# A residual attention block in fp32: the order of work in the front, before the loop reaches its steady state

## The chip, the cores and the metric

The kernel runs on one core of a Trainium2 chip. A core has five engines that work through their own lists of instructions in order and wait for one another by semaphores: TensorE (PE, with its weight loads shown as PEld), VectorE (DVE), ScalarE (ACT), GpSimd (POOL) and SyncE (SP), which here issues nearly all DMAs. The metric is the device time in microseconds (us); lower is better. "Span" is the part of a profiled execution between its first and its last instruction.

## The reference

There are 64 batches of 128 tokens with 512 features, all in fp32. Each batch goes through multi-query attention with 16 heads of width 64 and one shared key and value head, a learned null key and value, an additive bias per head and a mask; the result is projected, normed and added to the input.

```python
xn = layernorm(x, g_in)
q = (xn @ Wq).reshape(b, n, H, DH).transpose(0, 2, 1, 3) * scale
kv = xn @ Wkv
k, v = kv[..., :DH], kv[..., DH:]
k = concatenate([null_k, k]); v = concatenate([null_v, v])
sim = einsum('bhid,bjd->bhij', q, k) + bias      # null_attn_bias in column 0
sim = where(causal_mask, neg, sim); sim = where(mask_p, sim, neg)
attn = softmax(sim, axis=-1)
out = einsum('bhij,bjd->bhid', attn, v)
out = layernorm(out.reshape(b, n, INNER) @ Wo, g_out)
return x + out
```

## The kernel before

The order of the work is written out by hand: every engine executes its instructions in the order in which the program names them, and a tile's buffer is taken over when its last reader is done. The program is a front followed by `for n in range(-6, B - 1): step(n)` (L1222). A step works on several batches at once, each at another stage. In step n the q products of a group of four batches, the keys and values of batch n+6, the scores of batch n+2, the exponentials of batch n+1 and the attention times values of batch n are formed, and for older batches the output product, norm and residual.

**The front.** The loads of x_0 to x_3, of the gain vector, of wq in four parts and of wkv are issued first (L161 to L173). `norm_stats(m)` (L239) takes mean and variance on VectorE and the power of -0.5 on GpSimd; `norm_apply(m)` (L249) applies them, on VectorE for the first four tiles and on ScalarE afterwards (with a small product "nmr" on VectorE ahead of it); `norm_T(m)` (L261) makes four transposes on TensorE and a copy on ScalarE. `keep_busy(k)` (L1188) issues k products of the identity with itself, whose results nobody reads; each shows as two instructions in the profile. `weights_q(kc)` (L842) scales a quarter of wq by the gain, `weights_kv_prod(kc)` (L862) multiplies it by the null key on GpSimd, and `weights_kv(kc)` (L871) scales wkv and reduces that product to 16 further columns. `causal(u)` (L195) writes a large negative number into the bias where a key lies ahead of a query, on GpSimd. `load_bias(0)` writes rows that `causal(1)` has filled, so it waits for it. `aTb` (L224) is the buffer of the transposed attention; it is cleared once.

**The groups.** The first group's q is formed by plain products (`q_plain`, L370) in steps -6 to -3. From step -2 on, the next groups use a scheme with 7 products in place of 8: `weight_sums` and `weight_sum_3` (L384, L389) form sums of blocks of wq, `token_sum` (L392) sums of blocks of the transposed tokens on GpSimd, and `product`, `keep` and `q_out` (L406, L431, L435) multiply and put the parts together through the PSUM tiles "a", "c" and "w". In step -4 the keys and values of the first three batches are formed at once (L1180).

**Scores to values.** `bias_add(b)` (L458) puts bias plus mask into the tile S[b] on GpSimd, `null_copy` adds the two null columns, `scores` (PE) and `scores_add` (DVE) the products of q and k. `scores_max`, `exps`, `rinv` and `scale` are the softmax in two halves, on DVE, ACT, DVE and POOL. S has two buffers, so `bias_add(n+2)` can't start before S[n] was read by the transposes. For batches 0 and 1 these are done by TensorE (`attn_T_pe`, L606), for later ones by VectorE and DMAs. `values` (L647) starts the product with v; with it goes a one-element copy "done" on VectorE that later PE work waits for, and `values_end` finishes it. `out_mm(0)` (L689) is the plain output product of batch 0; `out_weight_sum` (L721) forms sums of wo's blocks on GpSimd in steps 0 to 3.

**DMAs.** `load_second` (L175), `load_bias(0)`, the mask and x loads inside the steps, and `load_late` (wo and the output gain, L209) go through SP's queue in program order. An x load waits until its buffer is free, and what stands behind it waits too.

Of the kernel before, what the change touches and what calls it, by code (L numbers as in the profile page):

```python
# [8 lines left out]
FP = mybir.dt.float32  # L9
# [8 lines left out]
def kernel(  # L18
# [59 lines left out]
    nc = tc.nc  # L78
# [60 lines left out]
    def load_mask(g):  # L139
        m8s[g] = gp.tile([P, TOK], U8, tag="m8", name=f"m8_{g}")  # L140
        nc.sync.dma_start(
            out=m8s[g],
            in_=mask[g * GB : (g + 1) * GB].rearrange("b n -> (b n)").partition_broadcast(P),
        )
# [28 lines left out]
    )  # L173

    def load_second():  # L175
        nc.sync.dma_start(out=nbh, in_=null_bias.partition_broadcast(P))
        nc.sync.dma_start(out=nvb, in_=cond[1].partition_broadcast(P))
        load_mask(0)
        for m in (4, 5, 6):
            load_x(m)  # L180
        load_bias(1)
        for r in range(2):
            nc.sync.dma_start(
                out=nv2[r * DH : (r + 1) * DH, :], in_=cond[1].unsqueeze(1)
            )

    def load_bias(u):
        rows = slice(u * DH, (u + 1) * DH)
        bias_r = attn_bias.rearrange("(u f r) i j -> u r i f j", u=2, r=2)[u]
        for r in range(2):  # L190
            rf = slice(r * NF, (r + 1) * NF)
            nc.sync.dma_start(out=biasp[rows, rf, 0:NL], in_=bias_r[r, 0:DH, :, 0:NL])
            nc.sync.dma_start(out=biasp[rows, rf, NL:], in_=bias_r[r, DH:N])
# [193 lines left out]
        nc.vector.tensor_tensor(s4, a12, s2, ALU.subtract)  # L387

    def weight_sum_3():  # L389
        nc.gpsimd.tensor_tensor(s3, a11, a21, ALU.subtract)  # L390

    def token_sum(g, k):  # L392

        xS[g, k] = gp.tile([P, GB // 2, HK, N], FP, tag=f"xS{k}", name=f"xS{k}_{g}", bufs=1)
        lo, hi = xT[g][:, 0 : GB // 2], xT[g][:, GB // 2 :]
        b11, b12 = lo[:, :, lo_k], hi[:, :, lo_k]
        b21, b22 = lo[:, :, hi_k], hi[:, :, hi_k]
        p, m = {
            1: (b12, b11),
            2: (b22, xS.get((g, 1))),  # L400
            3: (b22, b12),
            4: (b21, xS.get((g, 2))),
        }[k]
        nc.gpsimd.tensor_tensor(xS[g, k], p, m, ALU.subtract)  # L404
# [26 lines left out]
    def keep(tag, name):  # L431
        kept[name] = bp.tile([P, HT], FP, tag=f"k{name}", name=f"k{name}", bufs=1)
        nc.scalar.copy(kept[name], prod[tag])  # L433
# [26 lines left out]
    def bias_add(b):  # L460
        g, t = divmod(b, GB)
        if b in (B3 + 1, B3 + 4):
            S[b] = gp.tile([P, R8, ROW], FP, tag="xT", name=f"s_{b}")
        else:
            S[b] = sp.tile([P, R8, ROW], FP, tag="s", name=f"s_{b}")
        nc.gpsimd.tensor_tensor(  # L466
            S[b][:, :, 1 : ROW - 1],
            biasp,
            mneg[g][:, t].unsqueeze(1).broadcast_to([P, R8, NL + N]),
            ALU.add,  # L470
        )

    def null_copy(b):
        g, t = divmod(b, GB)
        nc.gpsimd.tensor_copy(  # L475
            S[b][:, :, 0 : ROW : ROW - 1],
            nv[g][:, t, DH:].rearrange("p (k e) -> p e k", k=2),
        )
# [58 lines left out]
    def rinv(b, hf):  # L537
        rinvs[b, hf] = small.tile([P, R8], FP, tag="rinv", name=f"rinv_{b}_{hf}")
        nc.vector.reciprocal(rinvs[b, hf], rsum[b][:, hf])
# [246 lines left out]
    def pair_pow(b):  # L786
        nc.gpsimd.tensor_tensor(yn[b][1], yn[b][1], nhalf, ALU.pow)
# [52 lines left out]


    def weights_q(kc):  # L842
        if kc < 2:
            nc.vector.tensor_scalar(
                wq[:, kc, :], wq[:, kc, :], gin8[:, kc : kc + 1], None, ALU.mult
            )
        else:
            nc.scalar.activation(
                wq[:, kc, :], wq[:, kc, :], AF.Copy, scale=gin8[:, kc : kc + 1]
            )  # L850
# [9 lines left out]
            )  # L860

    def weights_kv_prod(kc):  # L862
        prods[kc] = sp.tile([P, H, DH], FP, tag="s", name=f"prod_{kc}")
        nc.gpsimd.tensor_tensor(
            prods[kc],
            wq[:, kc, :].rearrange("p (h d) -> p h d", d=DH),
            nkb.unsqueeze(1).broadcast_to([P, H, DH]),
            ALU.mult,
        )
# [9 lines left out]
    def step(n):  # L879
        def ok(b, end=B):  # L880
            return 0 <= b < end

        qg, part = divmod(n + 6, GB)
        mkv, mk, mb = n + 6, n + 5, n + 11
        mns = [m for m in (n + 10, n + 12) if ok(m) and (m >= 2 * GB) == (m == n + 12)]
        q, f = ok(qg, NG), part
        last_g, last_f = divmod(n + 5, GB)
        fast, last = q and qg > 0, 0 < last_g < NG
# [21 lines left out]
        if second:  # L910
            if n != B3 + 1:
                out_sums(p5673)
        elif ok(nb) and n >= 0 and n != 1:
            bias_add(nb)
            null_copy(nb)
        if third:
            pair_pow(p4)
        for m in mns:
            norm_stats(m)
        if fast and f == 0 and fill:  # L920
            for k in range(1, 5):
                token_sum(qg, k)
            if n == -2:
                weight_sum_3()
        if n == -4:
            bias_add(0)
            bias_add(1)
        if ok(nb) and n < 0:
            null_copy(nb)
        if n == B3:  # L930
            blocks_T(B3 + 1)
            blocks_move(B3 + 1)
        if third:
            out_product(p4, 4, ps_y, "X", start=False)
        if one:

            out_mm(n - 1, 0, NF if n > B3 + 1 else NC)
            if n == 1:
                attn_T_pe(1)
                bias_add(nb)  # L940
                null_copy(nb)
                out_stats(0)
        if fast:
            if f == 0:
                q_tile(qg)
# [5 lines left out]
            scores_max(B3 + 1, 0)  # L951
        if last:
            product(last_g, last_f, 4, ps_q, "a", start=False)
        if soft:
            exps(eb, 0, 0, 4)
        if third:
            out_part(p4 + 1, 0, "X")
        if last:
            q_out(last_g, HC + last_f, lo_t, "a")
            product(last_g, last_f, 3, ps_q, "c", start=False)  # L960
            q_out(last_g, last_f, hi_t, "c", "u2")
        if n == B3 - 1:
            scores(B3 + 1, 1)
            scores_add(B3 + 1, 1)
            scores_max(B3 + 1, 1)
        if third:
            pair_stats(p4 + 1)
        if 2 * GB <= mb < B:
            tokens_T(mb)
            if (mb + 1) % GB == 0:  # L970
                tokens_out(mb // GB)
        if soft:
            exps(eb, 0, 4)
        if fast and f == 0 and not fill:
            token_sum(qg, 1)
        if soft and n != B3 + 1:
            rinv(eb, 0)
            scale(eb, 0)
        if third:
# [20 lines left out]
            product(qg, f, 2, ps_w, "w")  # L1000
        elif q and not fast:
            q_plain(qg, 2 * f)
        if soft:
            exps(eb, 1, 0, 2)
        if third and n != B3:
            pair_norm(p4)
# [19 lines left out]
        elif first:  # L1026
            out_keep("X", "yp1", "p1")
            out_product(p12, 2, ps_w, "w")
            out_part(p12, 0, "w", "yp1")
        if soft:  # L1030
            exps(eb, 1, 2, 4)
        if soft and not second:
            exps(eb, 1, 4, 6)
# [34 lines left out]
                mask_neg(qg)  # L1068
            out_part(p5673, 1, "Y", "yu2")
        if ok(n + 1) and fill:  # L1070
            exps(n + 1, 1)
        if one and n == 1:
            residual(0)
        if n == B3 - 1:
# [2 lines left out]
        if sc and n != B3:  # L1077
            scores(nb, 0)
            scores_add(nb, 0)
            if ok(n + 1) and fill:  # L1080
                rinv(n + 1, 1)
                scale(n + 1, 1)
        split = sc and n != B3
        if n == B3:
            pair_nmr(p4 + 1)
        if ok(n):
            values(n, split)
        if third and n != B3:
            pair_residual(p4 + 1)
            store(p4 + 1)  # L1090
# [4 lines left out]
        if not ok(n) and fast:  # L1095
            product(qg, f, 6, ps_q, "a", start=False)
            keep("a", "u2")
        if ok(n) and not split:
            values_end(n, split)
            if n > B3 + 1:  # L1100
                out_mm(n - 1, NF)
# [6 lines left out]
            store(p4 + 1)  # L1108
            scores_max(nb, 0)

        late = first and fast
        if sc:
            scores(nb, 1)
            scores_add(nb, 1)
            if not late:
                scores_max(nb, 1)
        if ok(n) and split:
# [50 lines left out]
            kv_out(mkv, pk[:, 0:KVN])  # L1168
        if ok(mk) and not ok(mkv):
            kT_out(mk, k_T(mk))  # L1170
        if n == -1:
            attn_T_pe(0)
        if n == B3 - 2:
            bias_add(B3 + 1)
            null_copy(B3 + 1)
# [17 lines left out]


    nc.vector.tensor_scalar(gin8, gin, DH**-0.5, None, ALU.mult)
    norm_stats(0)
    norm_stats(1)
    norm_apply(0)
    norm_T(0)
    norm_stats(2)  # L1200
    norm_apply(1)
    norm_T(1)
    norm_stats(3)
    norm_apply(2)
    norm_T(2)
    keep_busy(8)
    norm_apply(3)
    norm_T(3)
    keep_busy(10)
    load_second()  # L1210
    weights_q(2)
    weights_q(0)
    weights_q(3)
    weights_q(1)
    nc.gpsimd.memset(aTb, 0.0)
    for kc in range(2):
        weights_kv_prod(kc)
    nc.vector.tensor_scalar(vnb[:, 0:DH], nvb, -1.0, None, ALU.mult)
    null_order(vnb[:, DH:], nbh)
    causal(1)  # L1220
    load_bias(0)
    for n in range(-6, B - 1):  # L1222
        step(n)
        if n == -6:
            for kc in range(2):
                weights_kv(kc)
            for kc in range(2, KC):
                weights_kv_prod(kc)
            load_late()
        if n == -5:  # L1230
            for kc in range(2, KC):
                weights_kv(kc)
            causal(0)
            mask_neg(0)
            weight_sums()

    load_res(B - 1)
    store(B - 3)
# [47 lines left out]
```

## Time and profile before

| | |
|---|---|
| median of 3 runs | 1126.49 us (1124.78 to 1126.77) |
| profiled execution | 1125.21 us |
| its span | 1123.4 us |
| PE busy | 1086.8 us (97%) |
| DVE, ACT, POOL busy | 806.8, 678.2, 745.0 us |
| first q product on PE starts | 17.97 us |
| first product of step -2 on PE starts | 55.92 us |
| out_mm(0) in step 1 starts | 93.81 us |

In lists of waits, a row reads "engine, what waited, line <- engine, what released it, line: us in total, times, longest us". In the timeline a row is: start in us, length in us, engine, line, operation, tile written <- tiles read, shape, number of instructions merged into the row, and in brackets the idle time before it and what ended it. Overlapping starts in one queue are normal, since a row's length runs to the end of its last write. Tiles carry the program's names: x the tokens, pxT their transposes, xT the copy of these, pq and pa, pc, pw products for q, pk and pkv those for keys and values, ps scores, paU and paL the transposed attention, po the values, py the output.

### The profile page before, as it was taken

The page shows a single profiled execution, that of the slowest core. Times are in us where ns is not written, and L with a number is a line of the kernel's source. Part 1 is how long each engine was busy: PE and PEld are TensorE (multiplying, and loading weights), DVE is VectorE, ACT ScalarE, POOL GpSimd, SP SyncE. Part 2 cuts the span into 40 slices and gives each one's busy share as a digit, 9 for nine tenths or more (in the row PEclk, how much of TensorE's full clock was granted, in tenths as well). Part 3 has the DMA queues.
Part 4 walks back from the last instruction along what each step waited for, and adds up shares of the span by engine and source line. Part 5 has one row for each costly group of instructions (what it writes and reads, how often), then busy time and mean ns, then how long its engine had stood idle before and what let it go on. Part 6 is the DMA issues. An engine that isn't in the chain of part 4 may idle for free.

```text
span 1123.4 us, 27505 instructions
## 1 busy us (share of the span) xinstructions
PE 1086.8 (97%) x9780; PEld 872.6 (78%) x9780; DVE 806.8 (72%) x1741; ACT 678.2 (60%) x2710; POOL 745.0 (66%) x588
## 2 busy tenths in 40 slices
PE   6888999999999999999999999999999999999987
PEld 4465788888888888888888888788888888888643
DVE  6564677786787777778777777877777886666762
ACT  2345656666675666676565667566567756657661
POOL 5454877667675676767577676657768575777832
PEclk9999999999999999999999999999999999999999
DMA  6313244353444435345343634534353453422333
GB/s 186 123 33 97 66 132 122 88 163 97 136 127 126 118 91 169 101 125 135 123 123 92 167 104 125 130 120 117 101 163 103 127 134 108 104 77 77 96 104 103
DMA packets 107864, 130.09 MB, mean 116 GB/s; under 512 B 29264, under 2 KB 72528, under 8 KB 105936
## 3 DMA queue, kind: packets, MB, share of 16 engines
q1 hardware_dynamic: 106480, 126.96, 40.1%
q8 instruction: 78, 1.28, 0.5%
q10 hardware_dynamic: 1248, 1.38, 0.4%
q14 instruction: 58, 0.48, 0.1%
HBM read 54.86 MB, written 31.46 MB: 77 GB/s over the span
## 4 chain that ended last, share of the span: by engine, by line
PE 82%; DVE 4%; DMA 4%; ACT 3%; POOL 2%; SPq 2%; issue 1%; ACTq 0%; POOLq 0%; DVEq 0%
PE pa L422 17%; PE pyX L750 16%; PE pyY L750 8%; PE pc L422 8%; PE ps L495 8%; PE po L636 7%; PE pk L308 5%; PE pw L422 4%; PE pyw L750 4%; PE py L697 3%; ACT s L522 2%; DMA x<-in_x_dram 2%; SPq L601 2%; DMA nbh<-cond_null_attn_bias_dram 1%; POOL xS L404 1%
## 5 line engine op out<-in xcount | busy, mean ns | idle before, releaser
L522 ACT ACTIVATE s<-s,nmax 128x65 f32<-128x65 f32 (+1 forms) x1024 | 372.1, 368 | 0.4
L466 POOL TENSOR_TENSOR s<-biasp,mneg 128x1536 f32<-128x1536 f32 x64 | 221.1, 3456 | 109.5 <-DVE sb L575 98.1
L543 POOL TENSOR_TENSOR s<-s,rinv 128x512 f32<-128x512 f32 (+1 forms) x128 | 189.3, 1480 | 119.3 <-DVE nmro L794 91.4
L680 ACT ACTIVATE oT<-po,nv 128x512 f32<-128x512 f32 x128 | 81.1, 684 | 199.4 <-PE po L636 199.4
L522 ACT ACTIVATION_READ_ACCUMULATOR s<-s,nmax 128x1 f32 x1024 | 194.6, 190 | 0.0
L750 PE MATMUL pyX<-wT,oT 128*128 128x256 f32 x696 | 164.7, 379 | 0.5 <-DVE kyu L762 0.5
L750 PEld LDWEIGHTS pyX<-wT,oT 128*128 128x128 f32 x696 | 131.8, 190 | 19.6 <-DVE kyu L762 0.9
L495 PEld LDWEIGHTS ps<-kT,qT 64*64 64x64 f32 x4096 | 94.5, 135 | 46.4 <-DVE s L508 24.2
L508 DVE TENSOR_TENSOR s<-ps,s 128x512 f32<-128x512 f32 (+1 forms) x128 | 121.5, 949 | 9.0 <-PE ps L495 8.7
L422 PE MATMUL pa<-xS,wq 128*128 128x256 f32 x480 | 123.7, 380 | 2.0 <-POOL wq L390 1.0
L513 DVE TENSOR_REDUCE nmax<-s 128x8 f32<-128x520 f32 (+1 forms) x128 | 120.1, 939 | 5.1 <-POOL s L475 3.7
L495 PE MATMUL ps<-kT,qT 64*64 64x64 f32 (+1 forms) x4096 | 118.9, 252 | 3.8 <-DVE s L508 3.1
L636 PE MATMUL po<-aTb,vs 64*64 64x256 f32 (+1 forms) x1240 | 118.5, 382 | 2.3 <-DVE done L668 2.2
L575 DVE STREAM_TRANSPOSE sb<-s 128x1536 f32<-128x1536 f32 x62 | 110.0, 1774 | 12.9 <-POOL s L543 3.6
L433 ACT COPY ku<-pa 128x256 f32<-128x256 f32 x120 | 44.8, 373 | 93.2 <-PE pa L422 93.2
L422 PEld LDWEIGHTS pa<-xS,wq 128*128 128x128 f32 x480 | 86.7, 190 | 12.3 <-ACT ku L433 1.6
L308 PE MATMUL pk<-wkv,xT 128*128 128x144 f32 x488 | 69.9, 286 | 0.0
L443 DVE TENSOR_TENSOR qT<-pw,kp 128x256 f32<-128x256 f32 x60 | 25.4, 424 | 61.4 <-ACT kp L433 61.3
L422 PE MATMUL pa<-xS,wS 128*128 128x256 f32 x240 | 67.8, 405 | 0.0
L636 PEld LDWEIGHTS po<-aTb,vs 64*64 64x64 f32 (+1 forms) x1240 | 57.0, 135 | 12.8 <-issue 3.9
L246 POOL TENSOR_TENSOR rstd<-rstd,nhalf 128x1 f32<-128x1 f32 x64 | 35.8, 560 | 42.9 <-DVE rstd L245 42.8
L422 PE MATMUL pc<-xS,wS 128*128 128x256 f32 x240 | 61.9, 380 | 1.9 <-POOL xS L404 1.9
(120 smaller groups left out, 2101.1 us busy)
## 6 DMA issues: line engine op xcount, KB each, us to landing
aTb<-sb SPq DMA_DIRECT2D x369, 64.0 KB
x<-in_x_dram SPq DMA_DIRECT2D x64, 256.0 KB
res<-in_x_dram SPq DMA_DIRECT2D x64, 256.0 KB
out_dram<-y SPq DMA_DIRECT2D x64, 256.0 KB
aTb<-sb SPq DMA_DIRECT2D x492, 32.0 KB
xd<-xb SPq DMA_DIRECT2D x14, 1024.0 KB
xT<-xd SPq DMA_DIRECT2D x56, 256.0 KB
wo<-in_L_cond_Wo_dram SPq DMA_DIRECT2D x1, 2048.0 KB
```

The lines of the kernel that those rows point to most:

```text
L308: nc.tensor.matmul(pkv, xT[g][:, t, kc, :], wkv[:, kc, :], start=(kc == 0), stop=(kc == KC - 1),)
L422: nc.tensor.matmul(prod[tag], w[:, kc, f * P : (f + 1) * P], t[:, :, kc, :], start=(start and kc == 0), stop=(kc == HK - 1), skip_group_ch ...
L466: nc.gpsimd.tensor_tensor(S[b][:, :, 1 : ROW - 1], biasp, mneg[g][:, t].unsqueeze(1).broadcast_to([P, R8, NL + N]), ALU.add,)
L495: nc.tensor.matmul(pv[u * DH : (u + 1) * DH, r, f, :], qT[g][rows, f, t, hf, u], kT[b][rows, 0:nk], start=True, stop=True,)
L508: nc.vector.tensor_tensor(sv, pss.pop((b, hf)), sv, ALU.add)
L513: nc.vector.tensor_reduce(nmax[b][:, hf], S[b][:, :, WITH_NULL[hf]], AX.X, ALU.max, negate=True)
L522: nc.scalar.activation(row, row, AF.Exp, bias=nmax[b][:, hf, k : k + 1], accum_out=rsum[b][:, hf, k : k + 1],)
L543: nc.gpsimd.tensor_tensor(sv, sv, rinvs.pop((b, hf)).unsqueeze(2).broadcast_to([P, R8, sv.shape[2]]), ALU.mult,)
L575: nc.vector.transpose(sb.rearrange("p j e q -> p e j q"), S[b][:, :, 1 : ROW - 1].rearrange("p e (j k) -> p e j k", k=Q),)
L636: nc.tensor.matmul(pos[b][u][r * DH : (r + 1) * DH, half], vals[keys, b % GB, 0:DH], aT_of(b)[keys, slots, r * NF : (r + 1) * NF], start=s ...
L680: nc.scalar.activation(oT[b][:, u * NF : (u + 1) * NF, :].rearrange("p f (s q) -> p s f q", q=Q), po[u].rearrange("p h i f q -> p (h i) f q"),
L750: nc.tensor.matmul(prod[key], h[:, c, :], w[:, c, :], start=(start and c == 0), stop=(c == HC - 1), skip_group_check=not start,)
```

## The change

In words, from top to bottom of the diff:

- In `load_second`, x_4 to x_6 and the upper half of the bias are issued first; the mask, the null bias `nbh` and the null value `nvb` come behind them.
- `weight_sum_3` moves from GpSimd to VectorE, and in step -2 it and two of the token sums stand ahead of the norm of tile 10; the other two token sums stand behind `null_copy`.
- `weights_q` scales three of the four parts of wq on VectorE and one on ScalarE; before it was two and two.
- The four products of `weights_kv_prod` get a buffer each (two borrow buffers that are used later), and the last three follow one another in step -6. `causal(1)` and `load_bias(0)` come behind them.
- The norm of tile 6 is taken and applied at the end of step -5, ahead of the weight sums, in place of in step -4.
- In the steps -2 to 1, maxima, exponentials, reciprocals, scalings, bias adds and the transposes of batches 0 and 1 get other places in the order.
- In the front, 25 unread products (calls of 14, 4, 2, 2 and 3) stand among the first transposes; before it was 8 and 10 around the fourth one. `norm_stats(1)` follows `norm_T(0)`.
- Clearing `aTb` and `load_late` move behind step -4, and the null terms `vnb` to the end of step -5.

```diff
     def load_second():
-        nc.sync.dma_start(out=nbh, in_=null_bias.partition_broadcast(P))
-        nc.sync.dma_start(out=nvb, in_=cond[1].partition_broadcast(P))
-        load_mask(0)
         for m in (4, 5, 6):
             load_x(m)
         load_bias(1)
+        load_mask(0)
+        nc.sync.dma_start(out=nbh, in_=null_bias.partition_broadcast(P))
+        nc.sync.dma_start(out=nvb, in_=cond[1].partition_broadcast(P))
...
     def weight_sum_3():
-        nc.gpsimd.tensor_tensor(s3, a11, a21, ALU.subtract)
+        nc.vector.tensor_tensor(s3, a11, a21, ALU.subtract)
...
     def weights_q(kc):
-        if kc < 2:
+        if kc != 1:
             nc.vector.tensor_scalar(
...
     def weights_kv_prod(kc):
-        prods[kc] = sp.tile([P, H, DH], FP, tag="s", name=f"prod_{kc}")
+        pool, tag = ((sp, "s"), (sp, "s"), (hp, "sb"), (hp, "xb"))[kc]
+        bufs = None if kc < 2 else 1
+        prods[kc] = pool.tile([P, H, DH], FP, tag=tag, name=f"prod_{kc}", bufs=bufs)
...
-        mns = [m for m in (n + 10, n + 12) if ok(m) and (m >= 2 * GB) == (m == n + 12)]
+        mns = [
+            m
+            for m in (n + 10, n + 12)
+            if ok(m) and (m >= 2 * GB) == (m == n + 12) and m != 6
+        ]
...
-        elif ok(nb) and n >= 0 and n != 1:
+        elif ok(nb) and n > 1:
             bias_add(nb)
             null_copy(nb)
...
+        if fast and f == 0 and fill:
+            if n == -2:
+                weight_sum_3()
+            for k in range(1, 3):
+                token_sum(qg, k)
         for m in mns:
             norm_stats(m)
-        if fast and f == 0 and fill:
-            for k in range(1, 5):
-                token_sum(qg, k)
-            if n == -2:
-                weight_sum_3()
...
+        if fast and f == 0 and fill:
+            for k in range(3, 5):
+                token_sum(qg, k)
...
             if n == 1:
                 attn_T_pe(1)
-                bias_add(nb)
-                null_copy(nb)
-                out_stats(0)
...
-        if soft:
+        if n == 1:
+            exps(eb, 0)
+            rinv(eb, 0)
+            scale(eb, 0)
+            exps(eb, 1, 0, 4)
+            bias_add(nb)
+            null_copy(nb)
+            out_stats(0)
+        elif soft:
             exps(eb, 0, 0, 4)
...
+        if n == 0:
+            attn_T_pe(0)
+            bias_add(nb)
+            null_copy(nb)
...
         if ok(n + 1) and fill:
-            exps(n + 1, 1)
+            exps(n + 1, 1, 0, R8 if n == 0 else 2)
...
             scores(nb, 0)
             scores_add(nb, 0)
-            if ok(n + 1) and fill:
-                rinv(n + 1, 1)
-                scale(n + 1, 1)
...
         if ok(n):
             values(n, split)
+        if n == 0:
+            rinv(1, 1)
+            scale(1, 1)
...
+        if n == -1:
+            exps(0, 1, 2)
...
-        late = first and fast
+        late = fast and (first or n < 0)
         if sc:
             scores(nb, 1)
             scores_add(nb, 1)
+            if n == -1:
+                rinv(0, 1)
+                scale(0, 1)
             if not late:
                 scores_max(nb, 1)
...
-        if n == -1:
-            attn_T_pe(0)
...
     nc.vector.tensor_scalar(gin8, gin, DH**-0.5, None, ALU.mult)
+    keep_busy(14)
     norm_stats(0)
-    norm_stats(1)
     norm_apply(0)
     norm_T(0)
+    norm_stats(1)
     norm_stats(2)
+    keep_busy(4)
     norm_apply(1)
     norm_T(1)
     norm_stats(3)
+    keep_busy(2)
     norm_apply(2)
     norm_T(2)
-    keep_busy(8)
+    keep_busy(2)
     norm_apply(3)
     norm_T(3)
-    keep_busy(10)
+    keep_busy(3)
     load_second()
     weights_q(2)
     weights_q(0)
     weights_q(3)
     weights_q(1)
-    nc.gpsimd.memset(aTb, 0.0)
-    for kc in range(2):
-        weights_kv_prod(kc)
-    nc.vector.tensor_scalar(vnb[:, 0:DH], nvb, -1.0, None, ALU.mult)
-    null_order(vnb[:, DH:], nbh)
-    causal(1)
-    load_bias(0)
+    weights_kv_prod(0)
     for n in range(-6, B - 1):
         step(n)
         if n == -6:
+            for kc in range(1, KC):
+                weights_kv_prod(kc)
+            causal(1)
+            load_bias(0)
             for kc in range(2):
                 weights_kv(kc)
-            for kc in range(2, KC):
-                weights_kv_prod(kc)
-            load_late()
         if n == -5:
             for kc in range(2, KC):
                 weights_kv(kc)
             causal(0)
             mask_neg(0)
+            nc.vector.tensor_scalar(vnb[:, 0:DH], nvb, -1.0, None, ALU.mult)
+            null_order(vnb[:, DH:], nbh)
+
+            norm_stats(6)
+            norm_apply(6)
             weight_sums()
+        if n == -4:
+            nc.gpsimd.memset(aTb, 0.0)
+            load_late()
```

More of the change, by code (lines that the diff above doesn't have):

```diff
@@ L971, in step @@
                 tokens_out(mb // GB)
-        if soft:
+        if soft and n != 1:
             exps(eb, 0, 4)
@@ L975, in step @@
             token_sum(qg, 1)
-        if soft and n != B3 + 1:
+        if soft and n not in (1, B3 + 1):
             rinv(eb, 0)
@@ L1002, in step @@
             q_plain(qg, 2 * f)
-        if soft:
+        if soft and n != 1:
             exps(eb, 1, 0, 2)
@@ L1029, in step @@
             out_part(p12, 0, "w", "yp1")
-        if soft:
+        if soft and n != 1:
             exps(eb, 1, 2, 4)
```

## The prediction

> **What bounds the kernel.** I read the busy rows first, then TensorE (PE) in stretches of 40 us. The columns behind the first number are PE, weight loads, VectorE (DVE), ScalarE (ACT), GpSimd (POOL), granted clock, DMA share, GB/s.
>
> ```profile
> PE 1086.8 (97%) x9780; PEld 872.6 (78%) x9780; DVE 806.8 (72%) x1741; ACT 678.2 (60%) x2710; POOL 745.0 (66%) x588
> ...
> 0.00:40.00 40.00, 30.10 (x108) 17.58 (x108) 26.94 (x52) 11.43 (x17) 20.54 (x23) 1.00 0.67 202
> 40.00:80.00 40.00, 32.08 (x265) 22.57 (x265) 20.22 (x56) 16.32 (x54) 20.65 (x17) 1.00 0.13 37
> 80.00:120.00 40.00, 35.68 (x349) 25.87 (x350) 23.99 (x57) 21.72 (x96) 21.43 (x15) 0.96 0.28 77
> ...
> 160.00:200.00 40.00, 39.96 (x390) 33.58 (x385) 32.71 (x67) 26.26 (x101) 29.78 (x24) 1.00 0.51 143
> ```
>
> From 160 us on PE is busy for practically all of a stretch, so an earlier PE there ends the kernel earlier by as much. The front idles 22.1 us in its first 120. What is late there is told by PE's waits up to 140 us, in two parts:
>
> ```profile
> PE pxT L268 <- DVE x L253: 9.3, 3, 7.2
> PE pxT L268 <- ACT x L259: 2.9, 2, 2.2
> PE po L636 <- DVE done L668: 2.2, 1, 2.2
> PE pc L422 <- POOL xS L404: 1.9, 1, 1.9
> PE po L636 <- DVE qT L443: 1.6, 1, 1.6
> PE pa L422 <- POOL wq L390: 1.0, 1, 1.0
> PE pa L422 <- ACT ku L433: 1.0, 2, 0.5
> PE paU L610 <- POOL s L543: 0.9, 1, 0.9
> PE pc L422 <- DVE qT L443: 0.7, 1, 0.7
> PE pkv L308 <- DVE vs L324: 0.5, 1, 0.5
> PE pyY L750 <- POOL yS L730: 0.4, 1, 0.4
> ```
>
> Without the first row, which lies ahead of the first q product, these sum to 13.1 us. Two things are not in them: unread products that hold the fourth transposes back, and half clock. The timeline shows the first:
>
> ```profile
> 11.69 1.38 POOL L1215 MEMSET aTb<- 128x1536 f32 x1
> 11.77 1.57 DVE L253 TENSOR_SCALAR x<-x,mv,rstd 128x512 f32<-128x512 f32 x1 [0.44 <-POOL rstd L246]
> 12.36 3.10 PE L1192 MATMUL busy<-ident 128*128 128x128 f32 x16
> 15.30 0.60 PE L268 MATMUL pxT<-ident,x 128*128 128x128 f32 x4
> 15.73 2.40 PE L1192 MATMUL busy<-ident 128*128 128x128 f32 x20
> 17.97 7.03 PE L373 MATMUL pq<-xT,wq 128*128 128x512 f32 x16
> ```
>
> The memset holds VectorE up, PE works off 16 unread products ahead of transposes that were ready, and wq for the first q product is scaled on ScalarE only after that. Below, T(m) is norm_T(m) on PE, and the "lead" is by how much PE reaches a named instruction earlier than in this trace. Times are us from the span's start.
>
> **Up to the first q product (lead 4.1).** norm_apply(3) took 1.57 us beside the memset of aTb, against 0.54 for its three siblings; the memset leaves, so it ends at 12.3. Ahead of norm_T(3) stand 4 products (2.40/20 = 0.12 each warm) in place of 16: transposes at 12.55, 0.60 long, the copy (0.59) ends at 13.7. weights_q(2) starts on VectorE at 12.35 and takes 0.74 (row of L844) where ScalarE began it at 16.4. By the stretches of 1 us, 3.3 MB had moved by 12 us, more than the four x tiles and wq (3.1 MB), so wq is there. First q product at 13.9 against 17.97. The 28 products of keep_busy(14) cost 3.4 us warm and 6.7 at twice that, from 1.3, where ident is ready; PE has nothing else until 7.2. If all stay cold, T(1) to T(3) slip and q starts near 16.9; the lead at T(7) below then falls by only 0.8, because another engine sets T(7). Free of cost: norm_stats(1) behind norm_apply(0), since VectorE waited for x_2 until 8.31 anyway; weights_q(1) alone on ScalarE (1.14, done by 14.9), since its part is read last of the four, near 16.5.
>
> **Port.** The trace shows POOL holding VectorE up: a wkv scaling of 0.28 us took 2.42 behind a prod, a vnb copy 2.34 against 0.16, about two short VectorE operations slipping in between two POOL operations. The three prods now follow one another, with causal(1): prod(0) 14.6-16.9, pow(4) to 17.5, three prods of 2.35 and causal(1) of 1.7 to 26.6 with the slips. VectorE's wkv work for kc 0 and 1 (two scalings, two reductions of 1.21, four copies) is cut up by this to 26.6; then stats(5) 1.05, pow 0.55, nmr 0.2, ScalarE 0.81: T(5) at 29.4, PE having waited 1.1 (0.65 before). Lead 3.5. Putting prod 2 and 3 in other buffers takes away POOL's own idle time behind the reductions (1.74 and 1.38), nothing else.
>
> **DMAs moved.** On SP, x_4 to x_6 and the upper bias go ahead of mask, nbh and nvb; x_4 is issued near 7.8 instead of 9.77, and the small ones have until 32 us. load_bias(0) drops behind x_7 (which waits for T(4), 21.3) and behind causal(1), as before: its four DMAs issue 26.6-29.2 where they were 21.9-24.9. The other half of the bias landed 4.2 us after its last issue (17.05 to 21.25), so 33.4; without wo's 2 MB beside it perhaps sooner, by before's own bound (31.8 - 24.9) as late as 36. wo and gob move to about 38, behind x_9 and T(6); at the 409 GB/s of 32-34 us wo takes 5 us, so the moves of nulls queued behind it, near 44, are not held, and its first reader stands after 80.
>
> **Steps -5 and -4 (lead 3.2 at T(7)).** The tail of POOL and VectorE: causal(0) to 35.1, pow(6) 35.65, nmr(6), the three weight sums (3.7) to 39.5, stats(8), pow(8) to 41.2, two bias adds (6.85) to 48.0, then the moved memset (1.38), 49.4, pow(7), nmr, ScalarE: T(7) at 51.15 against 54.39. On PE, T(6) no longer waits (2.24 back), but kv_out(0) stands behind the sums and nmr(8) at 41.35, so the transposes of k wait from 39.8 to 41.9; q products of step -3 run 43.7-50.6, and T(7) waits 0.55. What T(6) stops waiting for is thus spent mostly on kv_out. The wkv work for kc 2 and 3 (3.4), mask_neg (0.6), vnb and null_order (0.4) and stats(6) (1.05), all on VectorE from 28.5, end at 34.0, hidden by the bias landing and causal(0); if the bias were there early, they would be the bound, 1.1 us sooner than 35.1.
>
> **Step -2 (lead +2.6).** Token sums 1 and 2 (1.27 each) no longer queue behind pow(10): they start when xT is copied (55.7 on before's clock, 58.42 then), so the product that waited 1.93 finds its operand. The last waited 1.02 for weight sum 3 on POOL (2.35); VectorE does it in 1.22 (rows L385 to L387) before the stats. Against this speaks the Trainium skill, "SBUF — State Buffer", section "SBUF: two separate sides": a VectorE operation with two SBUF inputs and a POOL operation that reads SBUF exclude one another for a whole instruction. The trace has single-input cases of it, none of this kind (L385 ran with POOL idle). By the rows alone step -2 gains 2.7. By the rule, sum 3 slips in after token sum 1, as waiting VectorE operations did, and token sum 2 ends 0.1 too late: 2.6. If token sum 2 goes first, stats(10) and the first score add are 1.25 later: 1.3. I take 2.6.
>
> **Steps -1 and 0 (lead +2.8).** scores_max behind q_out frees pc (0.7). attn_T(0) goes behind two products (1.8 us), so scale(0,1) is done when it starts; ScalarE's exps in two lots let the ku copy through. rinv(1,1), which stood before the "done" copy that PE waited 2.2 for, goes behind it. These are 4.3 us of waits (0.7, 0.45, 0.9, 2.2); kept back are 0.9 for the last ku copy ahead of step 0 and 0.5 where oT waits for exps(1,1) on ScalarE. bias_add(2) starts after attn_T(0) as before and ends at the score add that needs it.
>
> **Step 1 (lead +3.6).** Twelve exps and rinv/scale(2,0) run under out_mm(0) (6.87 us), where ScalarE stood idle 8.98 for q_out. That takes away the wait of 1.6, the 0.52 for ku, and what followed:
>
> ```profile
> 110.00:112.00 2.00, 2.00 (x26) 1.36 (x30) 1.04 (x4) 1.65 (x4) 1.43 (x1) 0.59 0.00 0
> 112.00:114.00 2.00, 2.00 (x35) 1.41 (x27) 1.49 (x1) 0.04 (x1) 2.00 (x3) 0.56 0.00 0
> ```
>
> (0.41 + 0.44) x 2 = 1.7 us lost to the clock after an idle stretch of 1.6. The Trainium skill, "TensorE: Matmul & The Clock Gate", section "HAM oscillation — how this bites in real kernels", asks for no idle gap above about 3.4 us; by that figure this gap would not have dropped the clock, and the 1.7 need not come back: sum 10.5 in place of 12.2. The trace shows the drop right behind the gap, so I count it, but the 2.2 us at 88 dropped nothing: such a drop may turn up at a new gap as well. POOL's bias_add(3) now follows scale(2,0) and ends about when the score add wants it.
>
> Sum: 3.2 + 2.6 + 2.8 + 3.6 = 12.2. The profiled execution took 1125.21 (span 1123.4): 1113.0; the runs' median is 1.3 above it, so 1114.3.
>
> **Rivals.** (a) The bias and POOL tail comes later than worked out: each us of landing behind 33.4 is a us at T(7). POOL's unbroken list and the 36 as late bound speak for it, wo's absence from the wires against. With 2.6 us there, 1.3 from the port in step -2 and 1.7 of clock lost at the longer gap, the gain is 6.6: 1120. (b) Everything hides: 13.1 + 4.1 + 1.7 = 18.9 is the ceiling, 1107.6; bias landing at 31 and no clock drop give about 15.5: 1111 or less. T(7)'s long tail speaks against. (c) Slower: the lower bias, now behind x_7 and causal(1), lands late; pow(6), the bias adds and every norm behind them queue on POOL. Each us costs one; it decides from a landing near 46, which the 4.2 us row makes unlikely. (d) No change: the tail eats exactly what the rest gives, a landing within 2.3 us of that point.
>
> **Numbers.** The case above 0.58, with its own range of 10 to 15 us (1111.5 to 1116.5); (a) 0.25, (b) 0.07, (c) 0.07, (d) 0.03. For 8 in 10 I go into (a) up to a gain of 6 and take in most of (b), a gain of 17: 1109.5 to 1120.5. Faster 0.90, same 0.03, slower 0.07, with 0.2% (2.3 us, about what a measurement can tell from no change) as the bound.
>
> **What would show it.** First q product near 13.9; norm_apply(3) at 0.54; T(7) near 51 with PE's waits in steps -5 and -4 on ACT x and DVE vs; no PE wait on POOL xS, POOL wq or DVE done; out_mm(0) of step 1 near 85; no granted clock below 1 near 100. It is wrong if T(7) comes after 53, or if waits beyond 120 us grow.

## The result and the profile after

| | before | after |
|---|---|---|
| median (lowest to highest) of 11 runs each | 1126.7 us (1124.78 to 1130.91) | 1120.93 us (1119.67 to 1124.13) |
| profiled execution, its span | 1125.21, 1123.4 | 1119.67, 1117.9 |
| first q product on PE | 17.97 | 13.83 |
| q products of step -3, T(7) | 47.52, 54.39 | 45.77, 52.64 |
| first product of step -1 | 66.82 | 62.09 |
| out_mm(0) in step 1 | 93.81 | 86.16 |

The ratio of the times is 0.9949 [0.9939, 0.9959]: the kernel became faster by 5.8 us, where 12.2 were forecast. 1120.93 lies just outside the range given.

The first two views of the changed kernel are the busy row and PE in stretches, with the columns as before.

```profile
PE 1088.6 (97%) x9794; PEld 875.1 (78%) x9794; DVE 808.8 (72%) x1743; ACT 676.5 (61%) x2709; POOL 743.0 (66%) x587
```

```profile
0.00:40.00 40.00, 34.38 (x134) 21.62 (x134) 29.22 (x62) 11.37 (x18) 20.73 (x25) 1.00 0.47 152
40.00:80.00 40.00, 36.76 (x337) 27.66 (x341) 24.46 (x61) 18.82 (x72) 22.45 (x17) 0.96 0.30 96
80.00:120.00 40.00, 37.36 (x385) 26.71 (x375) 22.81 (x51) 24.23 (x103) 27.10 (x21) 1.00 0.34 88
...
160.00:200.00 40.00, 39.97 (x339) 33.55 (x337) 28.03 (x63) 25.38 (x104) 31.55 (x25) 1.00 0.45 119
```

PE idles 11.5 us in its first 120 instead of 22.1. Four of the 10.6 us between these are no gain, since PE fills them with unread products (9.4 us of them in place of 5.5). The half clock of 80 to 120 is gone (1.00 in place of 0.96), and one has appeared in 40 to 80 (0.96 in place of 1.00). The waits of PE up to 140 us:

```profile
PE pkv L308 <- ACT xT L269: 3.9, 1, 3.9
PE pxT L268 <- DVE x L253: 1.5, 2, 1.0
PE busy L1214 <- POOL nhalf L216: 1.4, 1, 1.4
PE pc L422 <- DVE qT L443: 1.3, 2, 0.8
PE pa L422 <- ACT ku L433: 1.0, 2, 0.5
...
PE pkv L308 <- DVE vs L324: 0.4, 1, 0.4
PE pxT L268 <- ACT x L259: 0.4, 1, 0.4
PE pc L422 <- POOL xS L404: 0.4, 1, 0.4
```

The rows on wq, on "done" and on POOL's s are gone as forecast, and the one on xS is down from 1.9 to 0.4. The third row lies ahead of all work, where PE waits for the identity. The first row is new: PE waits 3.9 us for ScalarE's copy of xT. The list can't show what the loop does with the rest of the gain; that comes further below.

**The front up to the first q product** went as worked out. In the timeline norm_apply(3) takes 0.55, three parts of wq are scaled on VectorE at once, and PE goes from the fourth transposes through 6 instructions of unread products straight to q:

```profile
11.83 0.55 DVE L253 TENSOR_SCALAR x<-x,mv,rstd 128x512 f32<-128x512 f32 x1 [0.44 <-POOL rstd L246]
...
12.29 2.07 DVE L844 TENSOR_SCALAR wq<-wq,gin 128x1024 f32<-128x1024 f32 x3
...
12.52 0.63 PE L268 MATMUL pxT<-ident,x 128*128 128x128 f32 x4
...
12.99 0.83 PE L1214 MATMUL busy<-ident 128*128 128x128 f32 x6
...
13.83 6.71 PE L373 MATMUL pq<-xT,wq 128*128 128x512 f32 x15
```

**Steps -5 and -4.** The same view of 36 to 42 us:

```profile
36.00 0.60 PE L268 MATMUL pxT<-ident,x 128*128 128x128 f32 x4
...
37.56 0.68 DVE L241 BATCH_NORM_STATS2 st<-x 128x6 f32<-128x512 f32 x1
...
38.73 0.55 POOL L246 TENSOR_TENSOR rstd<-rstd,nhalf 128x1 f32<-128x1 f32 x1 [4.98 <-DVE rstd L245]
...
39.31 0.21 DVE L258 TENSOR_SCALAR nmr<-mv,rstd 128x1 f32<-128x1 f32 x1 [0.66 <-POOL rstd L246]
...
39.61 0.81 ACT L259 ACTIVATE x<-x,nmr,rstd 128x512 f32<-128x512 f32 x1 [4.30 <-DVE nmr L258]
...
40.33 0.56 ACT L380 COPY qT<-pq 128x512 f32<-128x512 f32 x1
40.80 0.58 ACT L269 COPY xT<-pxT 128x512 f32<-128x512 f32 x1
...
41.44 2.19 PE L308 MATMUL pkv<-wkv,xT 128*128 128x144 f32 x8 [3.86 <-ACT xT L269]
```

T(6) is 6.7 us earlier than before (36.00 against 42.73), and its transposes lie ready in PSUM by 36.6. But their copy stands on ScalarE behind norm_apply(8), and that waits, by way of nmr and pow(8), for stats(8), which VectorE reaches only after the three weight sums (33.91 to 37.65). ScalarE stands idle 4.3 us in front of norm_apply(8), and PE 3.86 for a copy of 0.58 us. The products that wait, pkv of batch 1, do not read that copy. In the program pxT, pkv and pkT share two PSUM buffers (pool `ps_w`); pkv of batch 0 has one, pxT(6) the other, and the copy is what sets it free. The products behind the gap run at half clock: 2.19 for eight, against 1.15 for eight at 36.43 in this trace. The stretches of 2 us show it, with the granted clock third from the end:

```profile
42.00:44.00 2.00, 1.84 (x8) 1.41 (x7) 0.34 (x2) 0.00 (x0) 2.00 (x2) 0.50 1.04 344
44.00:46.00 2.00, 1.75 (x10) 1.75 (x11) 0.43 (x3) 0.00 (x0) 2.00 (x1) 0.75 1.04 387
```

**The loop.** The product that turns the keys (L342) comes once in a step, so the time from one to the next measures the steps. From step 6 to 54 odd steps take 17.28 us and even ones 15.49, in both kernels alike; all that is above this lies in the steps 6, 10, 14, ... (each fourth one), apart from 0.2 us in all in the kernel before and 0.7 in the changed one. Step n is here the time that ends with its product of L342:

```
kernel          sum over 15.49 us of the 13 steps 6, 10, ... 54   the largest (step: us)
before           5.1     38: 1.63   18: 1.09   10: 0.83
after            7.7     18: 1.75   14: 1.13   46: 0.96   30: 0.93
```

The excess is a wait for the transposed attention. In step 1 mod 4, SP issues the 14 moves of aTb behind the 4 loads of xT and the loads of res and x of the previous step; the values product of the next step wants the last of these moves. In the timeline of the changed kernel, SP's issues (SPq) of two steps, with PE's product at the slip in step 18:

```profile
353.78 9.05 SPq L601 DMA_DIRECT2D aTb<-sb  x14
362.93 1.96 SPq L295 DMA_DIRECT2D xT<-xd  x4
364.93 0.43 SPq L126 DMA_DIRECT2D res<-in_x_dram  x1
365.41 0.61 SPq L120 DMA_DIRECT2D x<-in_x_dram  x1
...
369.88 11.27 SPq L601 DMA_DIRECT2D aTb<-sb  x14
```

```profile
384.00 0.43 PE L636 MATMUL po<-aTb,nv 64*64 64x256 f32 x2 [1.30 <-DMA aTb<-sb]
```

On SPq a row's length is the time that SP needs to issue, not that of the transfer. The view of this line gives minimum, median and maximum of one issue in ns:

```profile
L601 SPq DMA_DIRECT2D aTb<-sb x861: 513/594/2035, 105.2 to 1094.6; - x173
```

So 14 issues one behind the other take SP 9 us where nothing holds them, 9.05 in the first row, and 11.27 behind the 1.5 MB of loads. The last move landed 1.4 us behind its issue, by the completions that the trace records. In this program SP's DMAs use eight completion semaphores in turn, and a DMA waits for the one eight before it; here the sixth move was held 0.9 us until the x load had landed, at 375; another 1.0 lies in the second issue, which took 1.57. In 115 of the 130 such steps (13 in each of the ten traces) the trace names the x load as what ended this wait. The list of SP's waits has a row for it in 120 to 1000 us:

```profile
SPq L601 <- DMA x<-in_x_dram: 18.0, 17, 2.1
```

In the kernel before the row reads 10.7, 12 times. That the excess is this wait is seen step by step: wherever it is above 0.3 us, in all ten traces (the kernel before, the changed one and the eight further down), the values product starts 0.1 to 0.3 us after the last move has landed. The list of PE's waits names only a part of it.

At the slip shown there is something else as well. Each of these moves ends in 16 completions. Fifteen of the last move's came by 382.58, the sixteenth at 383.86, and PE waited for that one. From 381.60 to 382.67 a packet of 16 KB had been moved on a queue that the page lists with the kind "instruction" (packets, MB and share of 16 engines in 381.6 to 382.7):

```profile
q8 instruction: 1, 0.02, 6.1%
```

Of the moves of batches 3 to 56 in all ten traces, 408 sets have no packet of this kind near their end, and there the sixteenth completion comes at most 0.09 us after the fifteenth; in the other 132 it comes up to 2.0 us later. So in step 18 about 1.3 of the 1.75 us of excess go with this packet.

What follows step 54, 136 us, takes another 0.9; PE's waits on aTb in the last 104 us are 3.0 us in place of 0.3.

### The profile page after: what moved, and what is told of

Read it like the earlier page. It is cut to its first block, busy times and chain, and to the rows that moved or that the text cites. A ratio compares the mean times of both kernels' runs of the same rounds, so it can differ in the third digit from the quotient of the medians.

```text
span 1117.9 us, 27535 instructions
## 1 busy us (share of the span) xinstructions
PE 1088.6 (97%) x9794; PEld 875.1 (78%) x9794; DVE 808.8 (72%) x1743; ACT 676.5 (61%) x2709; POOL 743.0 (66%) x587
## 3 DMA queue, kind: packets, MB, share of 16 engines
q8 instruction: 78, 1.28, 0.5%
## 4 chain that ended last, share of the span: by engine, by line
PE 70%; DVE 7%; DMA 7%; SPq 6%; POOL 4%; issue 3%; ACT 3%; POOLq 0%; DVEq 0%; ACTq 0%
PE pa L422 15%; PE pyX L750 14%; PE pyY L750 7%; PE ps L495 7%; PE po L636 7%; PE pc L422 7%; DMA x<-in_x_dram 6%; SPq L601 4%; PE pk L308 4%; PE pw L422 3%; PE pyw L750 3%; PE py L697 2%; ACT s L522 2%; POOL s L466 1%; SPq L295 1%
## 5 line engine op out<-in xcount | busy, mean ns | idle before, releaser
L308 PEld LDWEIGHTS pk<-wkv,xT 128*128 128x128 f32 x488 | 63.4, 191 | 0.1
L804 ACT ACTIVATE yn<-y,nmro,rstdo 128x512 f32<-128x512 f32 x58 | 45.3, 782 | 29.2 <-DVE nmro L794 29.2
```

Of the source, the lines that this page charges most:

```text
L308: nc.tensor.matmul(pkv, xT[g][:, t, kc, :], wkv[:, kc, :], start=(kc == 0), stop=(kc == KC - 1),)
```

## The experiments

In what follows "lead" is, as in the prediction, by how much PE is ahead of the profiled execution of the kernel before; "excess" is the sum of the 13 steps above. Each is of one profiled execution, while times are medians, and ratios are against the kernel before on the same chip (1127.24 us for experiments 1 to 4, 1129.22 for 5 to 8). The profiled execution of the kernel before, 1125.21, is at the fast edge of its runs; so a column sets the gain of the medians against the lead at step 6, too.

```
kernel                        T(7)   lead at   excess   lead at   gain of     gain less
                              lead   step 6             the end   medians     lead at 6
changed kernel                 1.75    9.6      7.7       5.5       5.8        -3.8
copy first                     4.75   12.2      9.0       6.5       9.7        -2.5
norm 8 last                   -1.41    6.4      8.0       0.9       4.3        -2.1
front only                     0.43    0.8      6.7      -2.3      -1.2        -2.0
copy first, other borrow       5.53   13.0      9.7       7.9      11.8        -1.2
other borrow                   1.20    9.0      8.8       2.6       6.7        -2.3
steps only                     0.74    8.6      5.1       6.8       9.2         0.6
steps and buffers              0.18    8.0      5.8       5.7       9.7         1.7
steps and load order          -0.67    7.2      6.2       4.9       9.6         2.4
```

**1. The copy of xT(6) ahead of norm_apply(8).** Is it ScalarE's order alone that PE waits for?

```diff
         for m in mns:
-            norm_apply(m)
+            if m != 8:
+                norm_apply(m)
...
             norm_T(n + 10)
+        if n == -4:
+            norm_apply(8)
```

> Edit to the changed kernel: in step -4 norm_apply(8) is issued after norm_T(6), so ScalarE copies xT of tile 6 first. Theory A (ScalarE's order makes PE's 3.86 us wait): the wait for ACT xT goes, the next one is VectorE's kv_out behind the weight sums, about 1.5 us; q products of step -3 start near 42.2 in place of 45.77, no half clock there, time 1120.9 - 3.4 = 1117.5. Theory B (VectorE's weight sums are the bound, ScalarE's copy only comes last by a little): the start moves by under 1 us, time about 1120.5. If the loop takes leads back (theory L, see the steps-only kernel), the time moves by less than the start of step 2 does.

1117.54 us, ratio 0.9913 [0.9899, 0.9928]. The wait is gone; what PE then waits for is what the prediction had there, the values of the first keys behind the weight sums:

```profile
PE pxT L268 <- DVE x L253: 2.0, 2, 1.3
PE pkT L342 <- DVE vs L324: 1.4, 1, 1.4
```

The granted clock is 1.00 from 40 to 48 us, and T(7) gains 3.00. Of what the forecast lacks, this part is shown: the order of two instructions on ScalarE was worth 3 us at T(7) and 3.4 between the medians, and the intervals of the two ratios lie apart. But the lead of 12.2 at step 6 again ends at 6.5.

**2. norm 8 behind everything.** The rival cure takes stats(8) and norm_apply(8) out of the way altogether.

```diff
-            if ok(m) and (m >= 2 * GB) == (m == n + 12) and m != 6
+            if ok(m) and (m >= 2 * GB) == (m == n + 12) and m not in (6, 8)
...
+            norm_stats(8)
+            norm_apply(8)
```

The two new lines stand behind the keys and values of the first three batches.

> Edit to the changed kernel: both norm_stats(8) and norm_apply(8) go behind the keys and values of the first three batches in step -4. Theory A with the rest of the chain: neither the copy of xT 6 nor kv_out waits for that norm, q products of step -3 start near 40.7 in place of 45.77, T(7) near 47.6 in place of 52.64, time 1120.9 - 5 = 1116. Theory B (the weight sums themselves hold kv_out): start near 42.5, time about 1117.5. Theory L: the time moves by less than step 2 does.

1122.96 us, ratio 0.996 [0.9947, 0.9974]: a miss. It is no faster than the changed kernel, and T(7) comes 3.2 us later than there. In the timeline of this kernel, VectorE, POOL and PE:

```profile
34.22 4.34 DVE L385 TENSOR_TENSOR wS<-wq 128x1024 f32<-128x1024 f32 x1
38.59 4.33 DVE L386 TENSOR_TENSOR wS<-wS,wq 128x1024 f32<-128x1024 f32 x1
42.96 1.22 DVE L387 TENSOR_TENSOR wS<-wq,wS 128x1024 f32<-128x1024 f32 x1
```

```profile
34.03 7.81 POOL L466 TENSOR_TENSOR s<-biasp,mneg 128x1536 f32<-128x1536 f32 x2
```

```profile
44.68 0.45 PE L342 MATMUL pkT<-ident,ktok 128*128 128x128 f32 x1 [5.58 <-DVE vs L324]
```

In the changed kernel pow(8) kept POOL's two bias adds back until 39.25, after the weight sums. Without it they start at 34.03, and each holds a weight sum up: 4.34 and 4.33 in place of 1.22. The Trainium skill, "SBUF — State Buffer", section "SBUF: two separate sides", states this exclusion of a VectorE operation with two SBUF inputs and a POOL operation that reads SBUF for the whole of an instruction, and these rows agree with it; the prediction weighed it for step -2 and did not look at the weight sums. PE's idle 5.58 us was then followed by 6 us at half clock (0.50 from 44 to 50), which costs another 3. A wait that is taken away may have kept two engines apart.

**3. and 4. The front alone, and the steps alone.** The first has every part of the diff ahead of step -3 and none of the others, the second the reverse. Against the changed kernel the second reads:

```diff
     def load_second():
+        nc.sync.dma_start(out=nbh, ...); nc.sync.dma_start(out=nvb, ...); load_mask(0)
         ...
-        load_mask(0)
-        nc.sync.dma_start(out=nbh, ...); nc.sync.dma_start(out=nvb, ...)
...
-        if kc != 1:
+        if kc < 2:
...
-        pool, tag = ((sp, "s"), (sp, "s"), (hp, "sb"), (hp, "xb"))[kc]
+        prods[kc] = sp.tile([P, H, DH], FP, tag="s", name=f"prod_{kc}")
...
-            if ok(m) and (m >= 2 * GB) == (m == n + 12) and m != 6
+            if ok(m) and (m >= 2 * GB) == (m == n + 12)
```

with the front's own list, from keep_busy to load_late, as it was before.

> The change's part outside the steps (unread products, weight scaling, prods, memset, load order, norm of tile 6) with the steps of before and weight sum 3 on GpSimd. If the parts add up: lead of 1.75 at the start of step -2, kept to the end, 1126.7 - 1.75 = 1124.9; about 1 us better still if the waits of before in step -1 to 1 are shorter by themselves. If the front is worth nothing by itself (rival: everything it gives is lost at the waits for token sums, which are on another engine), 1126.5.

> The front of before with the steps -2 to 1 of the changed kernel and weight sum 3 on VectorE. If the parts add up: lead 0 at step -2, 7.7 to 8.3 at step 2. Theory P (a lead passes through the loop, and the 3 to 4 us lost after step 2 in the changed kernel's trace are chance waits for DMAs): 1126.7 - 8 = 1119 with a loss of anything from 0 to 3 in the loop, seen at other steps than in the changed kernel. Theory L (the loop takes leads back, because the transposed attention is moved by DMAs that don't follow PE): the lead at the end is 5 to 6 whatever it was at step 2, time about 1121, with the waits at the same steps (14, 18, 30, 46).

Front alone: 1128.39 us, ratio 1.0006 [0.9991, 1.0021]. Steps alone: 1118.03, ratio 0.9915 [0.9899, 0.9932], faster than both parts together. The front alone starts its q products 4.0 us earlier and has lost all but 0.4 of it at T(7), by the wait of experiment 1:

```profile
PE pkv L308 <- ACT xT L269: 3.9, 1, 3.9
PE pxT L268 <- DVE x L253: 2.0, 2, 1.6
PE pc L422 <- POOL xS L404: 1.9, 1, 1.9
```

The steps alone keep 8.6 of lead at step 6 and an excess of 5.1, that of the kernel before. The table splits there: with the new front the excess is 6.7 to 9.7, with the old one 5.1 to 6.2; by the medians the six kernels with the new front end 1.2 to 3.8 us short of their lead at step 6, the three with the old one 0.6 to 2.4 above it, and on each of the two chips by itself the order is the same. The interval of one ratio is up to 2 us to either side, and the runs of one kernel lie up to 6 us apart, so it is the split of the groups that counts, not a row. SP shows the same split: to issue the moves of these 13 steps it needs 141.6 to 143.6 us in the four kernels with the old front, that before among them, and 144.2 to 146.6 in the six with the new.

**5. to 8. What of the front goes with the excess?** Two things of the front last into the loop: other addresses of buffers (two prods borrow "sb" and "xb", whose place in SBUF shifts), and the order of the loads. Experiment 5 gives the steps alone the borrowed buffers, 6 takes them from the changed kernel (the prods go to wT), 7 takes them from the kernel of experiment 1, and 8 gives the steps alone the new order of the loads.

```diff
 # 5 (against the steps alone); 6 and 7 the other way, with wT
-        prods[kc] = sp.tile([P, H, DH], FP, tag="s", name=f"prod_{kc}")
+        pool, tag = ((sp, "s"), (sp, "s"), (hp, "sb"), (hp, "xb"))[kc]
...
 # 6 and 7
+        if kc < 2:
+            prods[kc] = sp.tile([P, H, DH], FP, tag="s", name=f"prod_{kc}")
+        else:
+            prods[kc] = wT[:, kc - 2].rearrange("p c (a d) -> p (c a) d", d=DH)
...
 # 8 (against the steps alone); load_second as in the changed kernel
-            load_late()
...
+        if n == -4:
+            load_late()
```

> The steps-only kernel (1118.0) plus one piece of the change's front: the tiles prod_2 and prod_3 borrow the buffers sb and xb, the order of work stays. Because these tags are then allocated first in their pool, sb, xb, y, vs, nv and kT lie at other SBUF addresses for the whole kernel (sb 195616 in place of 219424). Theory D (the loop loses about 3 us in kernels with the new front because of where these tiles lie): 1121, with waits for the moves of aTb in the loop. Theory O (the order of the DMAs in the front does it): 1118 or a few tenths better.

> The changed kernel (1120.9) with prod_2 and prod_3 in parts of wT, which is first written in step 0, in place of sb and xb: the order of work is the same, the tiles of the loop lie where they lay before. Theory D: 1118, lead at step 2 as in the changed kernel (9.5) and kept to the last score steps within 0.5. Theory O, or anything else of the front: 1120.9 with a loss of about 3 in the loop.

> Both edits: norm_apply(8) behind norm_T(6) as in e2a (1117.5) and prod_2 and prod_3 in wT. Theory D: 1114.7, lead at step 2 of 12.2 kept. Theory O: 1117.5.

> The steps-only kernel (1118.0) plus the change's load order alone: x_4 to x_6 and the upper bias ahead of mask, nbh and nvb, and wo and gob behind step -4. Theory D: 1118. Theory O (the order of DMAs in the front shifts how they meet in the loop): 1121, with waits for aTb in the loop.

5: 1119.51 us, ratio 0.9914 [0.9896, 0.9933]. 6: 1122.48, 0.9938 [0.9919, 0.9957]. 7: 1117.43, 0.9898 [0.9881, 0.9915]. 8: 1119.65, 0.9917 [0.99, 0.9935]. The borrowed buffers don't do it: with them the steps keep a small excess (5.8), without them the changed kernel keeps a large one (8.8). The order of the loads alone doesn't do it either (6.2). An early arrival at step 6 is not the cause either: the front alone arrives 0.8 us early and has 6.7, the steps alone 8.6 early and have 5.1. Nor does the row of SP's waits on the x load tell the kernels apart: it is 10.7 us before and 18.0 after, but 16.8 in the steps alone.

The traces show one thing that goes with the front: where a packet of 16 KB of the kind "instruction" meets the end of a batch's moves. In every kernel with the old front this is so in the steps 15, 19 and 37, in every one with the new front in 5, 23, 41 and 45, and in the five with both the new front and the new steps in 18 too. Of these, only 18 is a step whose moves stand behind the loads; there the last completion came 1.0 to 1.7 us late, and the excess of that step is 1.6 to 2.3 us, against at most 1.1 in the other five. No run moves this packet alone, so it is an observation and not a tested cause, and in the front alone, with an excess of 6.7, it is missing.

What of the front lengthens SP's issuing of the moves stays open. Issuing the loads of res and x of these steps from another queue, which would show whether the moves' place behind the x load is what costs, was not tried; nor was a further division of the front.

The version of experiment 7 has the lowest ratio: 1.02% below the kernel before. Its interval lies clear of that of the changed kernel, but overlaps those of experiments 1, 4, 5 and 8.

## Why the prediction was wrong

In the terms of its sum, by the profiled executions:

```
step                      forecast   measured   from
T(7)                        3.2        1.75     54.39 - 52.64
step -2                     2.6        2.98     lead 4.73 at step -1
steps -1 and 0              2.8        2.92     lead 7.65 at out_mm(0)
step 1                      3.6        1.94     lead 9.59 at step 6
the loop, 6 to 54           0         -3.13     lead 6.46 behind step 54
the last 136 us             0         -0.91     lead 5.55 at the end
sum                        12.2        5.55
```

**The step that failed most** is the premise that "an earlier PE there ends the kernel earlier by as much", which the prediction read from a busy row of 39.96 in 40. It put what the loop does with the lead at nothing, and the loop took back 3.1 us, the end 0.9. The premise is true of 36 of the 49 steps: all but two of them take the same time to within 0.1 us. It fails in each fourth one, in which PE waits for the last of the moves that SP issues behind the loads. It is no law of this loop: in the three kernels with the old front and the new steps leads of 8.6, 8.0 and 7.2 us at step 6 came through, as gains of 9.2, 9.7 and 9.6 between the medians. A share of busy time averages such steps out: PE is 97% busy in both kernels. The page's chain that ended last would have been a place to look; of after it says

```profile
PE 70%; DVE 7%; DMA 7%; SPq 6%; POOL 4%; issue 3%; ACT 3%; POOLq 0%; DVEq 0%; ACTq 0%
```

where before PE had 82% and DMA and SPq 6% together. That it is the new front and not the later steps that goes with this loss is shown by experiments 3 to 8 as a split of two groups; which of its parts does it is not.

**T(7), 1.45 short.** The prediction followed VectorE and POOL to nmr(8) and asked what PE does with kv_out; it did not write ScalarE's list beside them. There the copy of xT(6), whose PSUM buffer the next kv products need, stood behind norm_apply(8). The wait expected on the transposes of k at 39.8 to 41.9 came one stage earlier, on kv products of which a stage's work was still to do, and 1.5 us of half clock (half of 42 to 44, a quarter of 44 to 46) came on top. Two errors partly cancelled: the lower bias did not land at 33.4, causal(0) ran at 28.98 to 31.16 instead of up to 35.1, so the VectorE work of wkv and stats(6) was the bound, which the prediction had named for this case.

**Right.** The first q product (13.83 for 13.9), with norm_apply(3) at 0.55, though the 28 first products took 6.28 us, near the 6.7 of the slow case. Step -2: sum 3 on VectorE does go ahead of token sum 2, and token sum 2 is held, as the prediction had it by the rule of the two sides; in the timeline, VectorE and then POOL:

```profile
54.92 1.42 DVE L390 TENSOR_TENSOR wq<-wq 128x1024 f32<-128x1024 f32 x1
```

```profile
55.34 2.13 POOL L404 TENSOR_TENSOR xS<-xT,xS 128x512 f32<-128x512 f32 x1
```

2.13 in place of 1.27. In steps -1 and 0 the waits of 2.2 on "done" and 0.9 on s are gone, and qT, ku and oT hold PE up by 0.5 each: 2.92 for 2.8.

**Step 1, 1.7 short.** The clock came back as forecast: 1.00 from 98 to 104. The warning that such a drop may turn up at a new gap came true as well, at 42. But a wait of 0.8 on qT stands where 1.6 were taken away, the wait of 0.5 on ku is there as before, and 0.3 on s is new.

Rival (a) has the time, 1120, and not the mechanism: the bias was early, not late. The warning given at the end, "if waits beyond 120 us grow", is what came about.

## What to carry to other kernels

When an instruction on the critical engine is moved ahead, write out the list of every engine that its result passes, ScalarE's copies too, and look for one ahead of it that waits on something late. Before a gain in the front is counted at full value, measure single steps of the loop, not busy shares: here three in four are set by the bound engine and one by moves that have no slack. Read what a row of a DMA queue measures before it is called a transfer: 9 of the 10.5 us from the first issue to the last landing were SP's issuing. A wait taken away also lets loose what stood behind it, and on VectorE and POOL this can cost more than the wait (4.34 for 1.22 us, twice).

## What the runs showed of the hardware

An idle stretch of 3.86 us on PE was followed by half clock for some 4 us (0.50 and 0.75), one of 5.58 in experiment 2 by 6 us of 0.50; in the kernel before one of 1.63 was followed by 0.59 and 0.56, and one of 2.24 at 40.5 to 42.7 by none. The Trainium skill, "TensorE: Matmul & The Clock Gate", section "HAM oscillation — how this bites in real kernels", puts the limit at about 3.4 us: the stretches of 3.86, 5.58 and 2.24 agree with it, the one of 1.63 does not, so a gap below that figure may still cost clock.

The 14 moves of a batch carry 640 KB (8 of 32 KB and 6 of 64 KB), but what takes their time is SP: 0.59 us for one issue, 9.05 for all, and 1.4 more until the last has landed. Behind 1.5 MB of loads the issuing took 11.27: one issue took 1.57, and the sixth move waited 0.9 for the x load to land.

Beside a packet of 16 KB of the kind "instruction", 1.07 us long, the sixteenth completion of a move came 1.28 us after the fifteenth. Without such a packet near, these two lay at most 0.09 us apart in 408 sets of moves.
